# A mask's identity product cut into four column tiles, in the first cross attention of a two-layer perceiver

## The chip, the cores and the metric

The kernel runs on one core of one Trainium2 chip. The metric is the device time of one execution in microseconds. Profiled times below come from one execution taken by the hardware profiler; its engines are TensorE (PE, with its weight loads listed apart as PEld), VectorE (DVE), ScalarE (ACT), GpSimd (POOL) and SyncE (SP, which issues the DMAs).

## The reference, cut to what matters

Two batches of 256 tokens of width 256 attend to 4096 context rows. The reference is six residual blocks; the change lies in the first.

```python
x = x + xattn0(layernorm(x), ctx, ctx, mask)     # 16 heads of 16, the block of this change
x = x + conv_block(layernorm(x), ...)            # gates, two depthwise convolutions, linears
x = x + quantized_ffn(layernorm(x), ...)
x = x + xattn1(layernorm(x), ctx, ctx, mask2)    # one head of 256
x = x + attn1(layernorm(x), ...)                 # 16 heads of 64, rotary
x = x + experts(layernorm(x), ...)               # 8 experts, 2 per token

# xattn0
q, k, v = (proj(t, W, b) for ...)                # (batch, head, row, 16)
energy = q @ k.T / 4
energy = where(mask == 0, -1e9, energy)          # mask: 256 x 4096, the same for all heads
out = softmax(energy) @ v @ Wo.T + bo
```

## The kernel before, in words

The function `l0_xattn` handles the first cross attention in 16 units; a unit is one batch and one pair of heads (the loop's `u`, with `NU` = 16). In a unit there are eight blocks of 512 context rows (`j`) and two heads of the pair (`par`, the loop's `a`), so 16 steps a unit and 256 steps in all. Three units of work are interleaved in a step:

- `max_part` (L408) computes scores of a later unit with queries on the partitions, four products on row tiles (32 rows of the array, `tile_position=(r, 0)`), into a pair of PSUM banks `st`. `max_out` (L417, VectorE) adds the mask and reduces each query's maximum. `take_max` turns a unit's maxima into three bf16 pieces on POOL (L384, L389) and transposes them with two products `psM` (L398); ScalarE copies them to `msh`.
- `weights_part` computes the scores of the unit before with the context rows on the partitions, into two PSUM banks `sts[0]` and `sts[1]` (the tiles `sT`), one for each half h of the block's context rows (two chunks of 128 rows by 256 queries in a bank). Its first product (L423) brings the mask into `sts[0]`: the 128 x 128 identity in bf16 is the stationary operand, and 512 columns of `addT` (0 or a huge negative number) stream through. Then come two products with a stationary operand of ones (L430), one to each bank, that subtract the maximum, and eight products of keys and queries on row tiles (L440). ScalarE takes the exponential of both banks (L446). The second half's mask is a multiplication with `keep` on POOL (L451).
- `weigh` (L459) multiplies the exponentials `p` of the block before (same head, so two steps earlier) with the values: four products in column tiles (`tile_position=(0, c)`, 32 columns of the array each, 32 output partitions each), 256 columns wide in fp32. The trace records two loads and two matmuls for each of these products, so eight records a step, in two rounds of four.

The order on the engines is the program's order: the whole block runs in a manual schedule for TensorE, VectorE, ScalarE and POOL. In the main loop (from L617) a step first advances each generator in the list `slow`, which adds work of other kinds between the steps: key projections of the second batch (`psK`, L201), value projections (`psV`, L365), the maxima's transposes (`psM`, L398), the collection of a finished unit (`psC`, L472) and a few single products. All of these use the whole array. Then `next(part)` issues the mask's product. Then `interleave` takes turns between `max_part` and the rest of `weights_part`: two L408, two L430, two L408, eight L440. Last comes the weighing. So on TensorE the mask's product follows the weighing of the step before, or the slow work where a generator has some in this step, and it precedes L408.

PSUM holds three single banks (`ps1`), which serve `sT` and also `psK`, `psV`, `psM` and `psC` in turn, two pairs (`ps2`, the tiles `st`) and one bank for `av`. A step takes two of the three single banks, so its second bank is the one that the step before had as its first.

After the last unit's maxima are found, the loop runs both heads of a block in one step (two mask products one behind the other), and VectorE takes over the multiplication with `keep` (L449).

Of the kernel before, what the change touches and what calls it, by code (L numbers as in the profile page):

```python
# [18 lines left out]
P = 128  # L19
# [26 lines left out]
class Kernel:  # L46
# [106 lines left out]
    def l0_xattn(self):  # L153
        nc, T, tc = self.nc, self.T, self.tc
# [95 lines left out]
        addT = a1.tile([P, NJ, 2, S], BF16, name="addT")  # L250
# [16 lines left out]
        for j in range(NJ):  # L267
# [3 lines left out]
            if j == 2:  # L271
                for f in range(2):
                    ps = self.bank("psQ")
                    for k in range(2):
                        nc.tensor.matmul(
                            ps, lhsT=wq[:, k, f * P : (f + 1) * P], rhs=self.xnT[:, k, :], start=k == 0, stop=k == 1
# [143 lines left out]
            )  # L420

        def weights_part(qz, kst, msh, par, j, p, sts, on_vector):
            nc.tensor.matmul(  # L423
                sts[0], lhsT=self.identb, rhs=addT[:, j].rearrange("p a q -> p (a q)"), start=True, stop=False,
                skip_group_check=True,
            )
            yield
            for h in range(2):
                r = 64 * h + 32 * par
                nc.tensor.matmul(  # L430
                    sts[h], lhsT=oneb[r : r + 3, :], rhs=msh[r : r + 3, :].unsqueeze(1).to_broadcast([3, 2, S]),
                    start=h >= NADD, stop=False, tile_position=(r, 0), skip_group_check=True,
                )
            yield
            for a in range(2):
                for i in range(2):
                    for h in range(2):
                        r = 64 * h + 32 * par
                        n0 = j * S + a * P
                        nc.tensor.matmul(  # L440
                            sts[h][:, a * S : (a + 1) * S], lhsT=kst[r : r + 32, n0 : n0 + P], rhs=qz[r : r + 32, i, :],
                            start=False, stop=i == 1, tile_position=(r, 0), skip_group_check=True,
                        )
                yield
            for h in range(2):
                nc.scalar.activation(p[:, h].rearrange("p a q -> p (a q)"), sts[h], AF.Exp)  # L446

            if on_vector:
                nc.vector.scalar_tensor_tensor(p[:, 1], p[:, 1], BIG, keep[:, j], ALU.min, ALU.mult)  # L449
            else:  # L450
                nc.gpsimd.tensor_tensor(p[:, 1].bitcast(I32), p[:, 1].bitcast(I32), keep[:, j], ALU.mult)  # L451
# [165 lines left out]
        for g in range(8 * NU + 12):  # L617
# [21 lines left out]
            u2, j = divmod(g - 10, 8)  # L639
            u3, j3 = divmod(g - 11, 8)  # L640

            for a in range(2):
# [4 lines left out]
                for n in ([a] if u < NU else [0, 1] if a == 0 else []) if 0 <= u2 < NU else []:  # L647
                    p = pt[u2, j, n] = a2.tile([P, 2, 2, S], F32, name="p", tag="p", bufs=5)
                    if u < NU or n == 0:
                        sts = [self.bank("sT") for _ in range(2)]  # L650
                    else:
                        pair = self.bank2("st")
                        sts = [pair[:, h, :] for h in range(2)]
                    part = weights_part(qz[u2], kst[u2], msh[u2], n, j, p, sts, u >= NU)
                    next(part)
                    gens.append(part)
# [1296 lines left out]
```

## Time and profile before

| what | value |
|---|---|
| time of three runs, us | median 1053.68 (1049.66 to 1055.73) |
| the profiled execution, us | 1050.14 |
| its span, first to last instruction, us | 1048.4 |
| mean granted TensorE clock | 0.965 |
| busy: PE, PEld, us | 966.5 (92%), 581.7 (55%) |
| busy: DVE, ACT, POOL, us | 672.3 (64%), 480.1 (46%), 386.8 (37%) |
| L423, the mask's product | 246 records into `sT`, 96.8 us, 394 ns each |
| L459, the weighing | 2048 records, 168.0 us, 395 ns each |
| L440, keys by queries | 1968 records into `sT`, 207.1 us |
| L408, scores for the maxima | 1024 records, 190.6 us |
| idle time of PEld ahead of L423 | 79.1 us, 194 times, released by "issue" |

Busy times of TensorE count the time from a matmul's start to its modelled end; matmuls overlap, so the length of a record (394 ns) is more than what it takes of the engine. What a product takes is read from the start of one to the start of the next. "Issue" as a releaser means that nothing in the profile was waited for. A chain view gives the work that ended last, link by link; a stretch view gives the busy time of each engine between two times.

### The profile page before, as it was taken

What the parts mean: (1) busy time and instruction counts of PE and PEld (TensorE: products, weight loads), DVE (VectorE), ACT (ScalarE), POOL (GpSimd) and SP (SyncE); (2) the same over time, 40 slices, a digit from 0 to 9 for tenths busy, and PEclk for the clock granted to TensorE, in tenths of its full rate; (3) what the DMA queues carried; (4) which work ended last, traced back from release to release, by engine and by line L of the source; (5) the groups of instructions that cost most, each with busy time, mean ns of one, the idle gap of its engine ahead of it and who ended that gap; (6) DMA issues with size and microseconds to landing.
All of it is one profiled execution on the core that took longest, in us unless ns stands there. A gap on an engine that the chain in (4) does not pass through costs nothing.

```text
span 1048.4 us, 21101 instructions
## 1 busy us (share of the span) xinstructions
PE 966.5 (92%) x8384; PEld 581.7 (55%) x8390; DVE 672.3 (64%) x1315; ACT 480.1 (46%) x1009; POOL 386.8 (37%) x418
## 2 busy tenths in 40 slices
PE   6998899999999999999999989764999999997978
PEld 2654355555555665555555547543575676455745
DVE  3268956666677447777887797668565432877651
ACT  1533456666666344666566672223141121455511
POOL 3323477777777435777777400111000000000000
PEclk9998799999999999999999999986899999999999
DMA  8888344334432240222221009432253796000000
GB/s 290 265 246 269 100 113 122 109 95 131 112 92 49 65 126 27 51 53 52 52 62 42 2 3 366 160 102 83 79 178 94 249 410 211 1 1 1 1 1 21
DMA packets 57523, 117.57 MB, mean 112 GB/s; under 512 B 6224, under 2 KB 28880, under 8 KB 55376
## 3 DMA queue, kind: packets, MB, share of 16 engines
q1 hardware_dynamic: 57424, 116.22, 35.8%
q8 instruction: 66, 1.08, 0.4%
q14 instruction: 33, 0.27, 0.1%
HBM read 97.85 MB, written 18.35 MB: 111 GB/s over the span
## 4 chain that ended last, share of the span: by engine, by line
PE 81%; DVE 12%; ACT 2%; issue 2%; DMA 2%; POOL 1%; SPq 0%; POOLq 0%; DVEq 0%; ACTq 0%
PE av L459 12%; PE st L408 10%; PE sT L440 8%; PE sT L423 6%; PE psV L365 6%; PE psS L1339 5%; PE psK L201 5%; PE av L1371 5%; PE psP L1456 3%; DVE junk L417 2%; PE psC L472 1%; PE psO L1581 1%; PE psP L807 1%; PE psS L1504 1%; PE psT L1379 1%
## 5 line engine op out<-in xcount | busy, mean ns | idle before, releaser
L417 DVE CUSTOM_DVE_ANT_0 junk<-st,madd 128x1024 bf16<-128x1024 f32 x256 | 313.0, 1223 | 97.1 <-PE st L408 94.5
L451 POOL TENSOR_TENSOR p<-p,keep 128x512 int32<-128x512 int32 x236 | 302.7, 1285 | 135.5 <-ACT p L446 130.0
L446 ACT ACTIVATE p<-sT 128x512 f32<-128x512 f32 x492 | 267.2, 595 | 180.0 <-PE sT L440 169.0
L440 PE MATMUL sT<-qz,kst 32*128 32x256 f32 x1968 | 207.1, 328 | 0.0
L408 PE MATMUL st<-kst,qz 32*128 32x512 f32 x1024 | 190.6, 450 | 7.5 <-DVE mx L417 7.5
L459 PE MATMUL av<-p,v 128*32 128x256 f32 x2048 | 168.0, 395 | 3.3 <-ACT avs L669 2.4
L440 PEld LDWEIGHTS sT<-qz,kst 32*128 32x128 f32 x1968 | 155.7, 189 | 0.2
L408 PEld LDWEIGHTS st<-kst,qz 32*128 32x128 f32 x1024 | 78.0, 186 | 83.8 <-issue 64.2
L104 POOL TENSOR_TENSOR rsx<-ve,nhalf 128x1 f32<-128x1 f32 (+1 forms) x10 | 5.7, 574 | 276.8 <-DVE ve L103 276.8
L430 PE MATMUL sT<-msh,oneb 3*128 3x512 bf16 x492 | 100.4, 390 | 0.5 <-ACT msh L402 0.2
L423 PE MATMUL sT<-addT,identb 128*128 128x512 bf16 x246 | 96.8, 394 | 0.2 <-ACT p L446 0.2
L201 PE MATMUL psK<-ctx,wkv 128*128 128x512 f32 x128 | 66.4, 650 | 6.6 <-DMA ctx<-in_ctxT 6.6
L423 PEld LDWEIGHTS <-identb 128*128 128x128 bf16 x256 | 25.4, 101 | 80.2 <-issue 79.1
L188 POOL TENSOR_TENSOR part<-kf,part 128x512 f32<-128x512 f32 x32 | 41.9, 1309 | 70.2 <-DVE part L187 67.7
L459 PEld LDWEIGHTS av<-p,v 128*32 128x32 f32 x2048 | 42.9, 108 | 41.6 <-ACT avs L669 3.3
L365 PE MATMUL psV<-wkv,ctx 128*128 128x256 f32 x256 | 61.8, 389 | 0.0
L1371 PE MATMUL av<-w,pT 128*128 128x256 f32 x256 | 60.3, 381 | 1.1 <-ACT pT L1383 1.1
L1339 PE MATMUL psS<-w,qk 128*128 128x512 f32 x128 | 57.8, 603 | 0.0
L365 PEld LDWEIGHTS psV<-wkv,ctx 128*128 128x128 f32 x256 | 46.7, 190 | 15.0 <-issue 9.2
L187 DVE TENSOR_SCALAR part<-kf 128x512 int32<-128x512 int32 x32 | 13.6, 426 | 61.4 <-ACT kf L205 27.9
L1371 PEld LDWEIGHTS av<-w,pT 128*128 128x128 f32 x256 | 46.4, 190 | 7.3 <-ACT pT L1383 2.1
L205 ACT ACTIVATE kf<-psK,bqk 128x512 f32<-128x512 f32 x32 | 22.0, 688 | 51.7 <-PE psK L201 51.7
(308 smaller groups left out, 1265.8 us busy)
## 6 DMA issues: line engine op xcount, KB each, us to landing
ks<-part SPq DMA_DIRECT2D x64, 256.0 KB, 2.9
w<-in_m_w SPq DMA_DIRECT2D x32, 512.0 KB, 7.7
kst<-ks SPq DMA_DIRECT2D x30, 512.0 KB, 6.6
ctx<-in_ctxT SPq DMA_DIRECT2D x24, 512.0 KB, 4.6
w<-in_ctxT SPq DMA_DIRECT2D x16, 512.0 KB, 5.7
w<-in_ctx SPq DMA_DIRECT2D x16, 512.0 KB, 4.0
qz<-qs SPq DMA_DIRECT2D x64, 64.0 KB, 6.2
mi<-in_x_maskT SPq DMA_DIRECT2D x16, 256.0 KB, 4.2
```

What stands on the lines that cost most here:

```text
L201: nc.tensor.matmul(ps, lhsT=w[:, 0, k, f * P : (f + 1) * P], rhs=ct[:, k, :], start=k == 0, stop=k == 1)
L365: nc.tensor.matmul(ps[:, i, :], lhsT=ct[:, k, n0 : n0 + P], rhs=w[:, 1, k, :], start=k == 0, stop=k == 1)
L408: nc.tensor.matmul(st[:, h, :], lhsT=qz[r : r + 32, i, qc * P : (qc + 1) * P], rhs=kst[r : r + 32, c * 512 : (c + 1) * 512], start=i == 0, ...
L417: nc.vector.tensor_tensor_reduce(out=junk, in0=st, in1=madd[:, qc, c].rearrange("p h a k -> p h (a k)"), scale=1.0, scalar=-1e38, op0=ALU. ...
L423: nc.tensor.matmul(sts[0], lhsT=self.identb, rhs=addT[:, j].rearrange("p a q -> p (a q)"), start=True, stop=False, skip_group_check=True,)
L430: nc.tensor.matmul(sts[h], lhsT=oneb[r : r + 3, :], rhs=msh[r : r + 3, :].unsqueeze(1).to_broadcast([3, 2, S]), start=h >= NADD, stop=Fals ...
L440: nc.tensor.matmul(sts[h][:, a * S : (a + 1) * S], lhsT=kst[r : r + 32, n0 : n0 + P], rhs=qz[r : r + 32, i, :], start=False, stop=i == 1, ...
L446: nc.scalar.activation(p[:, h].rearrange("p a q -> p (a q)"), sts[h], AF.Exp)
L451: nc.gpsimd.tensor_tensor(p[:, 1].bitcast(I32), p[:, 1].bitcast(I32), keep[:, j], ALU.mult)
L459: nc.tensor.matmul(av[c : c + 32, :], lhsT=vf[:, o : o + 32], rhs=p[:, h, a, :], start=j == 0 and par == 0, stop=j == NJ - 1, tile_positio ...
L1339: nc.tensor.matmul(ps[:, h, :], lhsT=qk[:, k, t * P : (t + 1) * P], rhs=ctxT[t // 2][2 * i + h][:, k, :], start=k == 0, stop=k == 1,)
L1371: nc.tensor.matmul(av, lhsT=pT[:, c, :], rhs=cn[t // 2][i][:, c, :], start=i + c == 0, stop=i == 7 and c == 3)
```

## The change

The product of the mask with the identity is cut into four, each with 32 columns of the identity as its stationary operand and 32 partitions of the same bank as its output. Each streams the same 512 columns of `addT`. They carry a `tile_position` in the column direction, as the products of the weighing do. Nothing else is changed. Each of the 256 products becomes four, so TensorE's list grows from one load and one matmul to four loads and four matmuls at each place; the order of all other instructions stays as it was. In the changed kernel the product stands at L425, and later lines move by three.

```diff
         def weights_part(qz, kst, msh, par, j, p, sts, on_vector):
-            nc.tensor.matmul(
-                sts[0], lhsT=self.identb, rhs=addT[:, j].rearrange("p a q -> p (a q)"), start=True, stop=False,
-                skip_group_check=True,
-            )
+
+            for c in range(0, P, 32):
+                nc.tensor.matmul(
+                    sts[0][c : c + 32, :], lhsT=self.identb[:, c : c + 32],
+                    rhs=addT[:, j].rearrange("p a q -> p (a q)"), start=True, stop=False, tile_position=(0, c),
+                    skip_group_check=True,
+                )
             yield
```

## The prediction

> **What bounds the kernel now.** I read four views, in this order: the chain that ended last on the page, the busy time by stretches, the chain of one ordinary piece of the first cross attention, and the timeline of the same piece. The page's chain first:
>
> ```profile
> PE 81%; DVE 12%; ACT 2%; issue 2%; DMA 2%; POOL 1%; SPq 0%; POOLq 0%; DVEq 0%; ACTq 0%
> PE av L459 12%; PE st L408 10%; PE sT L440 8%; PE sT L423 6%; PE psV L365 6%; PE psS L1339 5%; PE psK L201 5%; PE av L1371 5%; PE psP L1456 3%; DVE junk L417 2%; PE psC L472 1%; PE psO L1581 1%; PE psP L807 1%; PE psS L1504 1%; PE psT L1379 1%
> ```
>
> The mask's product, L423, is 6% of the span and stands on the chain. The stretches say where TensorE is full (columns: PE, PEld, DVE, ACT, POOL busy, then the granted clock):
>
> ```profile
> 90.00:135.00 45.00, 39.61 (x346) 20.16 (x345) 39.69 (x54) 17.96 (x34) 21.09 (x21) 0.73 0.44 145
> 135.00:340.00 205.00, 204.96 (x2428) 110.24 (x2426) 134.23 (x244) 133.68 (x267) 151.19 (x145) 1.00 0.38 104
> 340.00:400.00 60.00, 59.93 (x537) 40.56 (x536) 27.89 (x51) 23.88 (x47) 24.10 (x38) 1.00 0.34 95
> 400.00:590.00 190.00, 187.73 (x2462) 106.31 (x2466) 147.88 (x274) 117.48 (x227) 139.37 (x134) 1.00 0.18 44
> ```
>
> From 135 to 590 us TensorE is busy throughout at full clock, and POOL, the next, has over a quarter free. One step in that stage, from the chain in order of time (start, length):
>
> ```profile
> 426.60 0.57 PE av L459 x8
> 427.17 0.32 PE sT L423
> 427.49 0.32 PE st L408
> 427.81 0.00 PE sT L430
> 427.82 0.12 PE sT L440 x2
> 427.94 0.12 PE st L408
> 428.06 0.24 PE sT L440 x5
> 428.30 0.57 PE av L459 x8
> ```
>
> A step is 1.69 us, all TensorE: weighing 0.57 in column tiles (32 columns of the array), mask 0.32 on the whole array, then 0.80 in row tiles. What lies in the 0.32 is told by a place where two mask products stand together:
>
> ```profile
> 592.04 0.38 PE L423 MATMUL sT<-addT,identb 128*128 128x512 bf16 x1
> 592.26 0.38 PE L423 MATMUL st<-addT,identb 128*128 128x512 bf16 x1
> 592.57 0.39 PE L430 MATMUL sT<-msh,oneb 3*128 3x512 bf16 x2
> ```
>
> Start to start is 0.22 (0.216 in the trace) behind its like, but 0.31 before a row tile. So 512 columns stream in 0.213 and **a change of shape costs 0.10**. The same 0.10 stands behind the last weighing round (start of its last four products to the mask 0.312, of which 0.213 is its stream, since the two rounds themselves start 0.24 apart) and behind the last L440 (0.205 to the weighing, 0.107 of it stream). Three changes a step: row to column, column to whole, whole to row.
>
> **The change part by part.** Each of 256 mask products becomes four loads and four products of 32 columns; nothing moves on other engines, no DMA is added, and the order of the rest stays.
>
> *Clean steps.* In the instruction order 180 of 256 products stand right behind the weighing; the trace shows 173 of them followed by a row tile, 162 of these between 135 and 590 us. There the column-to-whole change goes: 0.10, and 0.01 for the whole array's load. Added: the four start one behind another. The four tiles of a weighing round start 7 ns apart, so the last is 0.02 late. The loads can be hidden: the second round's loads start 26 ns after the first round's products, well before the 0.24 that they have. TensorE then saves 0.09: a step of 1.60.
>
> Is something else late then? The second of the two L430 products (h=1) needs the bank that ScalarE's first exponential of the step before frees. That exponential starts 0.37 after the last L440 starts and takes 0.60; a product held by ScalarE at 424.06 starts 0.05 after it; from there to the last L440 it is 0.58. That ring takes 1.60, so it allows 0.093 and no more. POOL takes 1.28 a step, VectorE 1.22: both fit in 1.60. I take 0.09 (from 0.08, if ring and tiles add up, to 0.11, if the stagger is hidden): 162 × 0.09 = **−14.6 us**.
>
> *Steps with whole-array work between.* In 59 steps of that stretch another product stands ahead of the mask: 11 psK (L201), 14 psM (L398), 14 psC (L472), 14 psV (L365), 6 single ones. One of these:
>
> ```profile
> 345.06 0.64 PE L459 MATMUL av<-p,v 128*32 128x256 f32 x8
> 345.63 2.00 PE L365 MATMUL psV<-wkv,ctx 128*128 128x256 f32 x8
> 347.46 0.38 PE L423 MATMUL sT<-addT,identb 128*128 128x512 bf16 x1
> ```
>
> The last psV starts 0.216 ahead of the mask: no change of shape between them. The changed kernel puts one there: whole to column, then column to row. No row shows whole to column; the three changes that are shown cost 0.10 each, and I take that, with 0.02 for the stagger and up to 0.03 for a load that now lies open (the first weighing round has 0.24 for a stream of 0.213). Below nothing it can't go, as the stream itself does not shrink. 0.13, with ends 0.10 and 0.15: 45 × 0.13 = **+5.9 us**. The 14 psM steps differ: there L430 already waits for ScalarE, to 424.06 where TensorE would be ready at 423.90, so the 0.13 lies in that wait. Against it, POOL's burst at each unit's head is continuous:
>
> ```profile
> 447.45 1.27 POOL L451 TENSOR_TENSOR p<-p,keep 128x512 int32<-128x512 int32 x1 [0.41 <-ACT p L446]
> 448.67 0.22 POOL L384 CAST parts<-nm 128x8 bf16<-128x8 f32 x1
> ...
> 449.94 3.81 POOL L451 TENSOR_TENSOR p<-p,keep 128x512 int32<-128x512 int32 x3
> ```
>
> The weighing at 451.14 needs the first of those three (to 451.21) and so is held about 0.1 now. Three steps of 0.09 less bring it 0.27 earlier, and POOL does not follow. Nothing to 0.25 a unit; I take 0.10: 14 × 0.10 = **+1.4 us**.
>
> *The rest.* Before 135 us (11 clean steps, clock 0.73, TensorE not full) I count half, **−0.5**. After 590 us ten pairs of masks stand among waits for VectorE: nothing, at most −1.
>
> Sum: −14.6 + 5.9 + 1.4 − 0.5 = **−7.8 us**. What follows the attention begins earlier by as much; its weights are asked for when the attention's space is freed, so they move along. The profiled execution took 1050.14 us (span 1048.4, 1.7 around it); the runs have a median of 1053.68, with 1049.66 to 1055.73. I count from midway, 1051.9, as neither is the better stand: **1044 us**.
>
> One rule of the Trainium skill speaks against it: "TensorEngine Tiling (Array Packing)", Instruction Overhead, gives each matmul some 60 cycles. Three more products would by it be an estimated 75 ns (60 cycles at the 2.4 GHz of "TensorE: Matmul & The Clock Gate"), and 221 × 0.075 = 17 us would turn the gain into a loss of 9. The weighing's tiles, 7 ns apart in the trace, don't bear it out.
>
> **The rivals.**
>
> 1. *Another engine's ring takes the gain.* If ScalarE's exponentials and the banks behind them turn in 1.65 instead of 1.60 (each wait in the ring 0.02 longer than the one case shows), clean steps save 0.04: −6.5 + 5.9 + 1.4 − 0.5, so 1052. For it: slack of L430 against that bank is only 0.09 now. Against: the ring is worked out from rows that agree with each other within 0.01.
>
> 2. *The gap stays* (the other side). If the 0.10 is not the change of shape but the weighing's own drain, or the new loads are not taken ahead because both sets of a tile are in use until the second round starts, clean steps lose their 0.02 of stagger and gain nothing: 162 × 0.02 + 5.9 + 1.4 = +10.5, so 1062. It decides from a saving under 0.04 in a clean step, where 162 of them no longer pay for 45 others. For it: every product behind a weighing in this trace has the 0.10. Against: inside the weighing eight loads in column tiles do run ahead, and 0.12 of stream is left for the new four after the second round has started.
>
> 3. *The four do not run abreast.* The weighing's tiles take 256 columns in 0.213, half the mask's rate. If four tiles together get no more elements a cycle than that, the mask takes 0.427: 221 × 0.213 − 7.8 = +39, so 1091. If products are limited by issue: the densest 2 us (from 924.4) hold 41, 49 ns each; three more at that price are 221 × 0.147 − 7.8 = +25, so 1077. Against: bytes are equal (four per column in 0.83 ns, two in 0.42), and 26 products a step at 49 ns fill only 1.27 of 1.60. The Trainium skill's rule above is of this kind. It decides from 0.035 more than one stream.
>
> 4. *The change does nothing of the kind*, because TensorE is not what ends these steps: then 1052. The stretches speak against it; I fold it into the first.
>
> **How the numbers follow.** Forecast 0.62 (its own range, by the bounds above: −13.0 to −2, 1039 to 1050), first and fourth rival 0.17, second 0.13, third 0.08. 0.5% is 5.3 us, about what a measurement of this kernel can tell from no change. Of the forecast 0.52 lies beyond it and 0.10 short of it; with the first rival's 0.17 that is 0.27 within 0.5%, and the others make 0.21 slower. The range that leaves out 2 in 10 goes from 1037 (the forecast's best on the lower of the shown runs) to 1062, the second rival.
>
> **What will show it.** Clean steps of 1.60 instead of 1.69, the first mask tile 0.22 behind the second weighing round's start instead of 0.31, row tiles 0.33 behind that. The mask 0.32 behind the last psV instead of 0.22. POOL and ScalarE idle less ahead of each operation; L430 may now show waits for ScalarE. I am wrong if the four mask tiles start more than 20 ns apart, if a clean step is over 1.65, or if steps with psV or psC lose more than 0.15.

## The result and the profile after

The changed kernel took 1042.54 us (median of 13 runs, 1039.43 to 1055.58) against 1051.67 for the kernel before (13 runs beside them): ratio 0.9914, 95% interval 0.9888 to 0.9941, so 9.1 us faster where 7.8 were worked out. One of the 13 runs (1055.58, at a mean granted clock of 0.949) is a slow one and does not count in the ratio. The profiled execution has a span of 1038.9 us, 9.5 less. Only 7.6 of these lie between the first and the last weighing (98.2 to 627.4 before, 96.6 to 618.2 after); 1.7 lie ahead of the first, where only three of the 256 mask products run. I count those 1.7 as spread between executions: two versions below that leave the steps behind the weighing as they were have their first weighing earlier still (96.4 and 96.1). From the last weighing to the end it takes 420.9 before and 420.7 after.

One clean step (its mask stands right behind a weighing), from the chain in order of time (start, length):

```profile
428.93 0.57 PE av L462 x8
429.50 0.22 PE sT L425 x4
429.71 0.32 PE st L408
430.04 0.01 PE sT L433
430.04 0.12 PE sT L443 x2
430.16 0.11 PE st L408
430.27 0.25 PE sT L443 x5
430.52 0.57 PE av L462 x8
```

Where the mask stood with 0.32 it stands with 0.22, one stream; all other pieces are as they were. Counted from weighing to weighing, the median clean step between 135 and 590 us goes from 1.693 to 1.588. And a place with whole-array work ahead of the mask (timeline, start, length):

```profile
337.65 0.64 PE L462 MATMUL av<-p,v 128*32 128x256 f32 x8
338.22 1.99 PE L365 MATMUL psV<-wkv,ctx 128*128 128x256 f32 x8
340.15 0.40 PE L425 MATMUL sT<-addT,identb 128*32 128x512 bf16 x4
```

From the first psV to the mask it is 1.93 where it was 1.83. The third place is the head of a unit; the lines stand in the order of their start:

```profile
445.46 2.52 POOL L454 TENSOR_TENSOR p<-p,keep 128x512 int32<-128x512 int32 x2
...
446.34 1.09 PE L462 MATMUL av<-p,v 128*32 128x256 f32 x8
446.49 1.09 ACT L449 ACTIVATE p<-sT 128x512 f32<-128x512 f32 x2 [0.50 <-PE sT L443]
446.80 0.14 PEld L462 LDWEIGHTS av<-p,v 128*32 128x32 f32 x4 [0.32 <-POOL p L454]
```

The same weighing in the kernel before:

```profile
451.14 0.76 PE L459 MATMUL av<-p,v 128*32 128x256 f32 x8
```

The weighing, 0.64 long elsewhere and 0.76 at this place before, has grown to 1.09: its second half starts 0.46 late, when the first of the two POOL operations is done (445.46 and some 1.29).

One more place got longer, and only once: VectorE normalises the rows of the next block (tile `h`), and TensorE transposes them into `psT`. The kernel before, first POOL, then VectorE and TensorE:

```profile
413.14 2.51 POOL L451 TENSOR_TENSOR p<-p,keep 128x512 int32<-128x512 int32 x2
414.50 1.62 DVE L720 TENSOR_SCALAR h<-x,mvx,rsx 128x256 f32<-128x256 f32 x2
415.95 0.78 PE L727 MATMUL psT<-ident,h 128*128 128x128 f32 x4 [0.81 <-DVE h L720]
```

and the changed kernel, with its stretch view behind (columns as in the prediction, the granted clock 0.52):

```profile
407.41 3.79 POOL L454 TENSOR_TENSOR p<-p,keep 128x512 int32<-128x512 int32 x3
408.78 2.57 DVE L723 TENSOR_SCALAR h<-x,mvx,rsx 128x256 f32<-128x256 f32 x2
410.23 0.30 PE L730 MATMUL psT<-ident,h 128*128 128x128 f32 x1 [0.85 <-DVE h L723]
411.41 0.55 PE L730 MATMUL psT<-ident,h 128*128 128x128 f32 x3 [0.88 <-DVE h L723]
...
413.00:416.50 3.50, 3.50 (x36) 1.92 (x38) 2.39 (x5) 1.59 (x4) 1.86 (x4) 0.52 0.00 0
```

POOL now has three multiplications one behind the other, both operations on `h` run beside them, and TensorE waits twice. That step is 1.3 longer, and the two behind it, at the lower clock, 1.3 more.

By medians over all such places of the two traces, from the start of the product ahead of the mask to the mask, and from there to the row tile behind it:

| what stands ahead | before, us | after, us | difference |
|---|---|---|---|
| weighing, from its last tile | 0.312 + 0.319 | 0.196 + 0.329 | -0.106 |
| psV (L365) | 0.216 + 0.309 | 0.309 + 0.329 | +0.113 |
| psC (L472) | 0.112 + 0.306 | 0.193 + 0.330 | +0.105 |
| psK (L201) | 0.429 + 0.309 | 0.523 + 0.330 | +0.115 |
| psM (L398) | 0.056 + 0.309 | 0.149 + 0.330 | +0.114 |

### The profile page after: what moved, and what is told of

Same layout as the page of the kernel before. It is cut to its first block, busy times and chain, and to the rows that moved or that the text cites. A ratio compares the mean times of both kernels' runs of the same rounds, so it can differ in the third digit from the quotient of the medians.

```text
span 1038.9 us, 22643 instructions
## 1 busy us (share of the span) xinstructions
PE 954.6 (92%) x9158; PEld 587.4 (57%) x9158; DVE 671.8 (65%) x1315; ACT 479.8 (46%) x1009; POOL 387.6 (37%) x418
## 4 chain that ended last, share of the span: by engine, by line
PE 81%; DVE 11%; issue 2%; ACT 2%; DMA 2%; POOL 1%; SPq 1%; POOLq 0%; DVEq 0%; ACTq 0%
PE av L462 12%; PE st L408 10%; PE sT L443 8%; PE psV L365 6%; PE psS L1342 5%; PE sT L425 5%; PE psK L201 5%; PE av L1374 5%; PE psP L1459 3%; DVE junk L417 2%; PE psC L475 1%; PE psO L1584 1%; DMA mi<-in_x_maskT 1%; PE psP L810 1%; PE psS L1507 1%
## 5 line engine op out<-in xcount | busy, mean ns | idle before, releaser
L462 PE MATMUL av<-p,v 128*32 128x256 f32 x2048 | 170.1, 396 | 3.5 <-ACT avs L672 2.4
L425 PE MATMUL sT<-addT,identb 128*32 128x512 bf16 x984 | 100.9, 389 | 0.2 <-ACT p L449 0.2
L201 PE MATMUL psK<-ctx,wkv 128*128 128x512 f32 x128 | 63.8, 628 | 6.3 <-DMA ctx<-in_ctxT 6.3
L365 PE MATMUL psV<-wkv,ctx 128*128 128x256 f32 x256 | 61.8, 389 | 0.0
L365 PEld LDWEIGHTS psV<-wkv,ctx 128*128 128x128 f32 x256 | 46.7, 190 | 15.0 <-issue 9.2
L425 PEld LDWEIGHTS <-identb 128*32 128x32 bf16 x1024 | 29.7, 97 | 36.3 <-issue 18.5
```

Source lines behind the costliest of these rows:

```text
L201: nc.tensor.matmul(ps, lhsT=w[:, 0, k, f * P : (f + 1) * P], rhs=ct[:, k, :], start=k == 0, stop=k == 1)
L365: nc.tensor.matmul(ps[:, i, :], lhsT=ct[:, k, n0 : n0 + P], rhs=w[:, 1, k, :], start=k == 0, stop=k == 1)
L425: nc.tensor.matmul(sts[0][c : c + 32, :], lhsT=self.identb[:, c : c + 32], rhs=addT[:, j].rearrange("p a q -> p (a q)"), start=True, stop= ...
L462: nc.tensor.matmul(av[c : c + 32, :], lhsT=vf[:, o : o + 32], rhs=p[:, h, a, :], start=j == 0 and par == 0, stop=j == NJ - 1, tile_positio ...
```

## The experiments

The theory: **TensorE pays about 0.10 us each time that the shape of its tiles changes**; the cut takes one such change from a clean step and adds one where whole-array work stands ahead. The rivals: it is the smaller loads that count, not the shape; the losses are elsewhere; and each product costs a time of issue.

### Column tiles only where the weighing stands ahead

```diff
     def bank(self, name):
+        self.whole = self.whole or name != "sT"
...
+            n = P if self.whole else 32
-            for c in range(0, P, 32):
+            for c in range(0, P, n):
...
-                    sts[0][c : c + 32, :], lhsT=self.identb[:, c : c + 32],
+                    sts[0][c : c + n, :], lhsT=self.identb[:, c : c + n],
...
         def weigh(av, vf, p, hp, par, j):
...
+            self.whole = False
```

> Column tiles only in the 180 places right behind the weighing; one whole-array product in the 66 to 69 places that stand behind other whole-array work. Theory (a change of shape costs 0.10 to 0.11 us): clean steps 1.59 as in the changed kernel, the mask 0.216 behind the last psV as before, so the 45 steps get back 0.114 each: 5 us under the changed kernel, about 14.5 under the kernel before, ratio near 0.986. Rival (the part of the gain that was missing went into rings of ScalarE and POOL, not into the added changes of shape): 9 to 10 us under the kernel before, ratio 0.991, as the changed kernel.

Measured: 1038.79 us against 1052.31, ratio 0.9866 (0.9823 to 0.9910). Clean steps take 1.589, and the places with psV have their old figures, 0.216 and 0.309. So the added changes of shape are most of what the changed kernel gives back.

The two were then run beside each other on one chip.

> The hybrid again, beside the changed kernel on the same chip. Theory (45 added changes of shape at 0.114, and 14 psM places): 5 to 6.5 us under the changed kernel, ratio to the kernel before 0.986. Rival (the difference of the first hybrid run to the changed kernel is the runs' spread): no difference.

> The changed kernel as it is, beside the hybrid. Theory: ratio to the kernel before 0.991 to 0.992, 5 to 6.5 us over the hybrid. Rival: as the hybrid.

Measured: 1040.66 (ratio 0.9858, 0.9818 to 0.9899) and 1047.39 (0.9933, 0.9900 to 0.9965), 6.7 us apart, with intervals that just fail to overlap. Between the first and the last weighing the two traces are 7.1 apart: 5.2 are the added changes of shape, 1.5 stand behind `psT`, where the clock fell in the changed kernel alone, and 0.4 at the heads of units. This version beats both kernels.

### Column tiles only where whole-array work stands ahead

Against the version before this:

```diff
-            n = P if self.whole else 32
+            n = P if not self.whole else 32
```

> Four column tiles only where whole-array work stands ahead of the mask, one product behind the weighing: the added cost alone. Theory: 45 steps by 0.114, and nothing to 0.11 in the 14 with psM: 5 to 6.6 us slower than before, ratio 1.005 to 1.006, clean steps 1.69. Rival (an added change is hidden by waits or not paid by the end): no difference, ratio 1.000.

Measured: 1057.35 against 1052.31, ratio 1.0055 (1.0024 to 1.0087). Clean steps are at 1.692, psV places at 0.309 and 0.329. So the cost exists by itself, 5 us, and the two halves add up: -13.5 and +5.0 give -8.5, where the whole change gave -9.1.

### Two column tiles of 64

Against the changed kernel, as in the experiments below where nothing else is said:

```diff
-            for c in range(0, P, 32):
+            for c in range(0, P, 64):
```

(and `c + 64` for `c + 32`).

> The mask in two column tiles of 64 columns instead of four of 32. Theory (any change of shape costs 0.10): the mask starts 0.33 behind the first product of the weighing's second round, clean steps at 1.69, dirty steps 0.11 longer than before; 5 us slower than before, ratio 1.005. Rival (the gain comes from smaller loads that run ahead of a whole-array load, not from the shape being that of the weighing): clean steps near 1.59, ratio 0.991 as in the changed kernel.

Measured: 1060.82 against 1052.31, ratio 1.0083 (1.0054 to 1.0111). One step of its chain in order of time:

```profile
433.44 0.57 PE av L462 x8
434.00 0.34 PE sT L425 x2
434.34 0.33 PE st L408
```

The mask is at 0.34, not 0.22, and clean steps take 1.708. These are column tiles with loads of their own too, yet nothing is gained: 64 columns are another shape than the weighing's 32. This refutes the rival of the loads. When the loads start is told by the timelines, first of this version, then of the changed kernel:

```profile
433.93 0.11 PEld L425 LDWEIGHTS <-identb 128*64 128x64 bf16 x2 [0.41 <-issue]
433.94 0.41 PE L425 MATMUL sT<-addT,identb 128*64 128x512 bf16 x2
```

```profile
429.10 0.12 PEld L425 LDWEIGHTS <-identb 128*32 128x32 bf16 x4
429.31 0.40 PE L425 MATMUL sT<-addT,identb 128*32 128x512 bf16 x4
```

Where the shape stays, the loads run 0.21 ahead of their products; where it changes, they start with them. The cost is not the length of the load, though: it is 0.09 to 0.10 ahead of loads of 0.09 (mask) and of 0.18 (row tiles). What the engine does in that time is not shown. A clean step is 0.015 longer than with the whole-array product, which I had put at nothing; that is 2.3 us of the 3.5 beyond the 5 expected.

### Eight products instead of four

```diff
-            for c in range(0, P, 32):
-                nc.tensor.matmul(
-                    sts[0][c : c + 32, :], lhsT=self.identb[:, c : c + 32],
-                    rhs=addT[:, j].rearrange("p a q -> p (a q)"), start=True, stop=False, tile_position=(0, c),
+            for a in range(2):
+                for c in range(0, P, 32):
+                    nc.tensor.matmul(
+                        sts[0][c : c + 32, a * S : (a + 1) * S], lhsT=self.identb[:, c : c + 32],
+                        rhs=addT[:, j, a], start=a == 0, stop=False, tile_position=(0, c),
...
```

> The changed kernel with each of the four column products cut into two of 256 columns: eight loads and eight products in place of four, the same stream. Theory (the streams bound it, products in column tiles are issued 7 ns apart): a clean step longer by 0.03 at most, 0 to 6 us over the changed kernel, ratio to the kernel before 0.991 to 0.997. Rival (each product costs a fixed time of issue of some 25 ns): 4 x 0.025 x 221 = 22 us over the changed kernel, ratio 1.012.

Measured: 1043.52 against 1053.40, ratio 0.9920 (0.9887 to 0.9953), as the changed kernel. Clean steps: 1.587; mask to row tile 0.332 instead of 0.329. By the rule of the Trainium skill, "TensorEngine Tiling (Array Packing)", Instruction Overhead, four more products would be an estimated 0.1 us a step (some 60 cycles each, priced as in the prediction); no part of that is seen where products stand in column tiles.

### No mask product at all

This version leaves the mask of the first halves out of the weights.

```diff
-            for c in range(0, P, 32):
-                nc.tensor.matmul(sts[0][c : c + 32, :], ...)
...
-                    start=h >= NADD, stop=False, tile_position=(r, 0), skip_group_check=True,
+                    start=True, stop=False, tile_position=(r, 0), skip_group_check=True,
```

> The additive mask of the first halves is left out of the weights (no product at L425; the product of ones starts that bank). Theory with the ring (last L440, exponential of h=0, the bank, L430 of h=1, last L440: 1.59 to 1.60): clean steps stay near 1.59 although TensorE has 0.21 to 0.33 less to do, and L430 of h=1 waits some 0.2 for ScalarE; dirty steps lose 0.21 against before; 162 x 0.10 + 45 x 0.21 + some 3 = 29 us under before, ratio 0.972. Rival (TensorE alone bounds a step, so that the changed kernel has no ring near): clean steps 1.38, 162 x 0.32 + 45 x 0.21 = 61 us under before, ratio 0.942.

Measured: 1027.47 against 1052.31, ratio 0.9760 (0.9703 to 0.9816): 25 us, near the 29 and far from the 61. So clean steps have little left to win from TensorE. But the reason is only half as I put it:

```profile
411.98 0.57 PE av L455 x8
412.55 0.32 PE st L408
412.88 0.13 PE sT L426
413.01 0.12 PE sT L436 x2
413.13 0.02 PE st L408
413.14 0.34 PE sT L436 x5
```

L426, the product of ones, now waits 0.13 for ScalarE, so the ring of ScalarE that the prediction worked out binds; yet it turns in 1.49 to 1.50 (the median of 162 clean steps is 1.495), not in 1.59. From the last L436 to the exponential it takes 0.273 and no longer 0.367: when the second bank's product is held, the L436 of the first bank run ahead of those of the second, and the exponential, which needs the first bank alone, starts 0.09 sooner. The ring gives way by 0.1 when it is pushed. With a step shorter by 0.1 still, more than 25 us should have come. One loss is seen in the trace: from 495 to 509 us the granted clock is 0.51, where the kernel before has 1.00 throughout this stage, which makes an estimated 7 us (14 × 0.49). Why the clock fell is not shown, and the other losses were not separated.

### The five small operations at a unit's head, off POOL

To see whether POOL's burst is what the weighing waits for, these were moved to VectorE, in the first version above and in the kernel before.

```diff
-            eng = nc.vector if u == NU - 1 else nc.gpsimd
+            eng = nc.vector
```

> The hybrid (column tiles right behind the weighing, one product elsewhere) with the five small operations at each unit's head (L384, L389) moved from POOL to VectorE. Theory (faster steps bring the weighing to POOL's burst at a unit's head 0.3 earlier, and POOL does not follow; that is what 14 units lose, 0.28 each in the changed kernel): the weighing's wait of 0.45 at the unit's head goes, the two steps around psM take 3.5 instead of 3.85, 14 x 0.3 = 4 to 5 us under the hybrid, some 18 us under the kernel before, ratio 0.983. Rival (VectorE's five operations, 0.17 to 0.19 each and one of 1.2 in the one place where they ran there, delay the maxima and with them L408): no gain or a loss against the hybrid, ratio 0.987 or above.

> The kernel before with the same five operations on VectorE: the control. Theory: at 1.69 a step the weighing waits only 0.12 for POOL at a unit's head, and the wait of L430 for ScalarE takes over part of it: 0 to 1.7 us faster, ratio 0.998 to 1.000. Rival (the burst costs as much before the change as after): 4 to 5 us faster, ratio 0.996.

Measured: 1070.70 against 1053.40, ratio 1.0178 (1.0144 to 1.0213), and 1086.12, ratio 1.0313 (1.0271 to 1.0355). Both theories of mine on the gain missed, and so did the rival in the second; the rival in the first, VectorE late, had the sign. The timeline of the second, first POOL:

```profile
430.01 1.27 POOL L451 TENSOR_TENSOR p<-p,keep 128x512 int32<-128x512 int32 x1 [1.81 <-ACT p L446]
431.70 1.28 POOL L451 TENSOR_TENSOR p<-p,keep 128x512 int32<-128x512 int32 x1 [0.42 <-ACT p L446]
```

and VectorE:

```profile
430.37 0.95 DVE L384 CAST parts<-nm 128x8 bf16<-128x8 f32 x1
431.36 0.17 DVE L389 TENSOR_TENSOR rest<-nm,parts 128x4 f32<-128x4 f32 x1
431.56 0.18 DVE L384 CAST parts<-rest 128x8 bf16<-128x8 f32 x1
431.78 1.23 DVE L389 TENSOR_TENSOR rest<-rest,parts 128x4 f32<-128x4 f32 x1
433.04 0.18 DVE L384 CAST parts<-rest 128x8 bf16<-128x8 f32 x1
```

The small operations that start within a POOL operation end 0.03 to 0.04 behind it (431.32 behind 431.28, 433.01 behind 432.98); those that start in POOL's idle time take 0.17 to 0.18. So these operations on four or eight elements a partition wait out POOL's multiplications, the five take 2.85 together (430.37 to 433.22), and the maxima behind them start that much later. The experiment says nothing on POOL's burst.

### The same operations spread over three steps

```diff
                 if i < 2:
...
                     nm = rest
-            yield
-            yield
-            yield
+                yield
```

> The hybrid with the five small POOL operations of a unit's head spread over three steps (two, two and one) instead of all at once; psM stands where it stood. Theory (POOL's burst holds the weighing at a unit's head: 1.25 at once against 0.31 of idle time a step): the backlog stays under 0.5, the weighing's wait of 0.45 goes or falls under 0.1, some of it comes back as L430's wait for ScalarE, 0.2 to 0.3 less a unit, 14 units: 3 to 4 us under the hybrid, ratio to the kernel before 0.983. Rival (POOL's total, not its burst, is late, or psM waits instead for the last piece): no gain against the hybrid, ratio 0.987.

> The kernel before with the same spreading: the control. Theory: the weighing waits 0.12 there and L430 takes that over; 0 to 1.7 us faster, ratio 0.998 to 1.000. Rival (the burst costs as much before the change): 3 to 4 us faster, ratio 0.997.

Measured: 1041.98 against 1054.39, ratio 0.9888 (0.9860 to 0.9916), and 1058.25, ratio 1.0040 (1.0017 to 1.0064). No gain: the first is 0.002 to 0.003 behind the two runs of its base, within their intervals, and the second is 0.004 slower than the kernel before, with an interval clear of 1, where neither of its expectations had a loss. The weighing's wait did go, but psM waits in its place (waits of the first, in a window of 12 us around a unit's head):

```profile
PEld L398 <- POOL parts L386: 1.3, 1, 1.3
PE psM L398 <- POOL parts L386: 0.8, 1, 0.8
```

The last of the five now stands behind another multiplication, and the step with psM takes some 2.71 instead of 2.26 in the late units. The rival named there, psM waiting for the last piece, is what happened. That POOL sets the head of a unit, where the weighing waits, is shown by the waits; a version that takes it away was not found.

## Why the prediction was right

The forecast had the mechanism, the sign of each term and the steps in which each falls; its total is nearer than its terms. The two traces can be set beside each other step by step, from weighing to weighing. Between 136.7 and 590.5 us of the trace before (the stage in which TensorE is full):

| steps | forecast, us | measured, us |
|---|---|---|
| clean, 160 of 162 | -14.4 | -16.0 |
| with whole-array work ahead of the mask, 44 of 45 | +5.7 | +4.9 |
| with psM, 13 of 14 | +1.3 | +2.0 |
| with psT, and the two clean ones behind it | 0 | +2.7 |
| sum | -7.4 | -6.4 |

- **Clean steps**: the median fell by 0.105 where I took 0.09. The size was off by the stagger. The 0.312 of the prediction runs from the last of the weighing's four tiles to the mask, not from the first. I added 0.02 for the four tiles, but the weighing's own four had been late by the same 0.02 ahead of the whole-array product. Each mask tile follows the weighing tile on its own columns 0.216 later, so the stagger is paid once, as before.
- **The ring** was worked out at 1.60 and stands at 1.588 in the trace after (0.367 + 0.598 + 0.051 + 0.572, by medians). The second product of ones starts 0.051 behind the exponential in the median step, where it had 0.143 before, and 17 ns behind the first, where it had 3. So the ring is just reached, and holds that product by some 0.014. It was not the hard bound I took it for, as the kernel without the mask shows.
- **Steps with whole-array work**: 0.105 to 0.115 against 0.13. Ahead of the mask 0.08 to 0.09 are added, behind it 0.02, of which the stagger is 0.010; nothing of a load lies open.
- **Heads of units**: I gave 0.10 to each of 14 units. In seven of the 13 steps the loss is 0.2 to 0.33, in the other six it is nothing, so the sum, 2.0 against 1.3, is near by an average that no unit has. Where the weighing waits for POOL in the late units, it waits some 0.33 longer (from 0.13 to 0.46), more than the 0.25 that I had as the upper end, and the wait of L430 that was to hide the added change of shape gives way: with one product in these places (the first version above) the step grows by 0.18, in the changed kernel by 0.29.
- **The place with psT** had no term. I looked for what ScalarE and POOL do to the steps and not for what POOL does to VectorE. The trace of the changed kernel run again beside the first version repeats it (+2.7). All eight traces with clean steps of 1.59 or less have that step longer than the kernel before, by 1.1 to 2.1; the four others, at 1.69 to 1.71, by 0.1 at most. No version was run that removes it.
- **Outside this stage** I counted -0.5 ahead of it. The traces have -1.4 from the first weighing to 136.7 us, but the control with the spread operations, whose mask product is as before, has -1.8 there, so this is not owed to the change. After 590.5 us it is +0.2, where I took nothing.
- **The sum** in this stage is 1.0 short of the forecast. The medians give 9.1, with 6.2 to 11.8 by the interval, and 7.7 on another chip. The forecast of 7.8 lies among them, but in part by luck: the errors had opposite signs, and the largest, psT, was not thought of. Its range, -13.0 to -2, is also not what its ends add up to (-14.8 to -3.2).
- **The rivals**: the gap did not stay, the four run abreast (starts 7 ns apart in clean steps), and the ring takes some 0.014 of a clean step at most. Both the gain and the loss in the 44 steps came from the shape, as the one-sided versions show.

The section Key Properties of "TensorEngine Tiling (Array Packing)" in the Trainium skill says that changing the tiling mode, not just the tile, drains TensorE. The traces agree in that a change costs time, and give the price: 0.09 to 0.10 us a change at full clock, for changes between row tiles, 32 columns, 64 columns and the whole array.

## What to carry to other kernels

Count the changes of tile shape along TensorE's order, not only the products: at full clock each cost about 0.1 us here, as much as 256 columns take in one pass (0.109 from one half to the next in the version with eight products), and a product may be cut into tiles for no other reason than to have its neighbour's shape. Do that only in the places where the neighbour has that shape; where something else stands between, the same cut costs what it earned. And when a step gets faster, look for the wait that was almost there, on every pair of engines: POOL's burst held the weighing by 0.13 at 1.69 a step and by 0.46 at 1.59, and VectorE's two operations for psT, 1.62 long at 1.69 a step, took 2.57 at 1.59 because POOL had work beside both.

## What the runs showed of the hardware that was not expected

- Column tiles of 64 do not share a shape with column tiles of 32: 0.34 for the mask against 0.22.
- Cutting a column-tile product of 512 columns into two of 256 costs nothing measurable (0.332 against 0.329).
- VectorE operations on four or eight elements a partition took up to 1.23 us beside a POOL operation of 1.28, and 0.17 to 0.18 in POOL's idle time. The operation on `h` (128 x 256) took 0.4 to 0.5 where POOL was idle and up to 1.35 beside it. The section Who interferes with whom of "SBUF — State Buffer" in the Trainium skill says that the two engines share a pair of ports that one of them holds for a whole instruction; the ends within 0.04 of POOL's agree with it.
- In the changed kernel TensorE had work for 0.77 of the 2.50 us from 409.0 to 411.5, and from 413.0 to 416.5 its granted clock was 0.52. The version with eight products waits as long there and keeps its clock (the step is 1.3 longer, the two behind it are not).
